# Expert ranking in one comparison and one product per 16 tiles, and four heads' scores in one group in the last attention steps

## The chip, the cores and the metric

The kernel runs on one core of a Trainium2 chip. The core has five engines that run their own instruction queues: PE (TensorE, matmuls; its weight loads are listed as PEld), DVE (VectorE), ACT (ScalarE), POOL (GpSimd) and SP (SyncE, which here only issues DMAs). The metric is the device time of one execution in microseconds. The kernel before took 4520.11 us as the median of three runs (4519.01 to 4522.6).

## The reference, cut to what matters

A macaron block over x of 4 x 2048 x 256, float32: a half feed-forward, an attention and another half feed-forward, each behind a layer norm and added to its input.

```python
x = x + 0.5 * _L0_ffn_ref(_layernorm(x), gate_w, w1, w2)
x = x + _L0_attn_ref(_layernorm(x), Wq, Wk, Wv, Wr, Wo)
x = x + 0.5 * _L0_ffn_ref(_layernorm(x), gate_w, w1, w2)
```

The feed-forward is a mixture of 8 experts of width 256. The router, for 8192 tokens:

```python
probs = softmax(xf @ gate_w.T)                  # [N, 8]
order = argsort(-probs); p_sorted = probs in that order
csum = cumsum(p_sorted); reached = csum >= 0.9, the last one always
k_idx = argmax(reached)                         # experts up to here are assigned
R = p_sorted - rank where assigned, else -1e9   # rank is 1 for the likeliest expert
keep = the 1024 tokens of largest R, per expert
scores_sel = probs where assigned and kept, else 0
```

The attention has 16 heads of 16 dimensions with causal masking; each head also has 4 "nodes" with softmax probabilities. They give rotary positions (running sums of the probabilities), and the score of two tokens has the logarithm of the product of their node probabilities added before the softmax.

## The kernel before, in words

Tokens are cut into 64 tiles of 128 rows. `experts` runs twice (before and after the attention), `attention` once; the three stages follow one another.

**The experts' first part** is a loop over groups of four tiles (line 303). `begin` loads 512 rows over SP's queue and takes their mean and variance on DVE (`bn_stats`, lines 185 and 186). `finish` normalises them (two of four tiles on ACT, line 206, and two on POOL, line 201), stores them by SP to the scratch tensor `normed`, transposes them on PE (line 215), copies the transposes out on ACT (line 219), multiplies them with the gate weights on PE (line 222) and copies the eight logits per token out (line 226). `spread` transposes these into `logits` (line 231), one group of tiles later.

After 16 tiles, `rank` works on 16 tiles at once: a softmax over 8 experts (maximum, difference, exponential on ACT, sum, reciprocal, product), and then, for each expert, which experts stand ahead of it. For that, each tile's 8 probabilities are written twice in a row: `twice` by POOL (lines 256 and 257), and `above` by DVE, with the second copy a hair larger (lines 258 and 259), so that ties fall as in the reference. Eight shifted windows of `above` are compared with the probabilities (line 263, DVE, eight instructions of 128 elements per partition for 16 tiles), and each result is multiplied by the shifted window of `twice` (line 266, POOL, eight instructions). `select` sums over the shifts (line 277: how many stand ahead; line 287: their summed probability), compares with the threshold and writes each token's key into `by_row` (line 293). It also cuts the probabilities into three bfloat16 parts on POOL (lines 280 to 285). `rank` is called in the loop at t = 16, 32 and 48 for 16 tiles each, at t = 60 for 12 tiles, and after the loop for the last 4 tiles; each `select` follows one round later. When all keys stand, PE transposes `by_row` (line 342) and a search of 14 rounds finds the key of rank 1024 per expert.

In this part the order of the instructions is not written out: a planner lists instructions engine by engine from their dependencies and its own estimates of cost; on the chip every queue is then worked off in that order. DVE, ACT and POOL thus stand still when the next instruction in their list waits.

**The attention** works in units of one sequence and four heads (16 units). A unit has four blocks of 512 queries, and a block has steps over tiles of 128 keys: `turns` lists them; the diagonal ones are the first (512 columns, masked), "two" (two pieces of 384 and 128 columns) and "one" (256 columns). A unit has 36 steps. `run` (line 1435) writes out the order by hand. In step n, for each of two pairs of heads, it issues

- `scores` of step n+1 for that pair (line 1077): two heads, each with a contraction of 32 rows of the array and a PSUM bank of its own, of the tag "sc", which has two buffers;
- `take`, the row maxima for later work, for the other pair (`maximum`, line 1144): two more heads in the other 32-row strips, with banks of the tag "mx", which has three buffers; DVE reads them;
- `weights`: the exponentials of the pair on ACT (`ex`), masked on POOL where the block is diagonal;
- `summed` (line 1103, into `acc`) and `summed_weights` (line 1120, into `den`) of step n, for half of the nodes and half of the columns, over all four heads;
- pieces of queued work (`normalise`, `project`, and the next unit's preparation), each of which takes one "mx" bank at a time.

`Metered` and `Clock` keep the planner's books for the queued work: an estimated time per engine, from which it decides which piece goes into which half step. `left` holds the maxima that are still to be taken; these run ahead of the scores, and `take` does nothing when its list is empty.

Of the kernel before, what the change touches and what calls it, by code (L numbers as in the profile page):

```python
# [14 lines left out]
ALU = mybir.AluOpType  # L15
# [4 lines left out]
P = 128  # L20
# [5 lines left out]
NX, FF = 8, 256  # L26
# [68 lines left out]
def macaron_kernel(  # L95
# [12 lines left out]
    nc = tc.nc  # L108
    N = x.shape[0]
    S = N // B  # L110
    NT = N // P
# [38 lines left out]
    def bcast(ap, shape):  # L150
        return ap.to_broadcast(shape)


    def experts(source, dst, base):

        GQ = min(4, ST)
        CH = 16
        V = 6
        full = [P, NT, NX]
        with tc.tile_pool(name="ffn", bufs=1) as pool, tc.tile_pool(  # L160
# [68 lines left out]
            def spread(t, turned):  # L229
                for i in range(4):  # L230
                    nc.tensor.transpose(
                        logits[:, t + i, :], turned[:, i * P : (i + 1) * P], ident[0:NX, 0:NX]
                    )

            def rank(c, m):

                some = [P, m, NX]
                pc = prob[:, c : c + m, :]
                one = pool.tile([P, CH], F32, name="one", tag="one", bufs=2)[:, 0:m]
                nc.vector.tensor_reduce(one, logits[:, c : c + m, :], AX.X, ALU.max)  # L240
                nc.vector.tensor_tensor(
                    pc, logits[:, c : c + m, :], bcast(one.unsqueeze(2), some), ALU.subtract
                )
                nc.scalar.activation(pc, pc, AF.Exp)
                nc.vector.tensor_reduce(one, pc, AX.X, ALU.add)
                nc.vector.reciprocal(one, one)
                nc.vector.tensor_tensor(pc, pc, bcast(one.unsqueeze(2), some), ALU.mult)

                ahead = pool.tile([P, CH, NX, NX], F32, name="ahead", tag="ahead", bufs=2)[:, 0:m]
                held = pool.tile([P, CH, NX, NX], F32, name="held", tag="held", bufs=1)[:, 0:m]
                twice = pool.tile([P, CH, 2 * NX], F32, name="twice", tag="twice", bufs=2)[:, 0:m]
                above = pool.tile([P, CH, 2 * NX], F32, name="above", tag="above", bufs=2)[:, 0:m]
                nc.gpsimd.tensor_copy(twice[:, :, 0:NX], pc)
                nc.gpsimd.tensor_copy(twice[:, :, NX:], pc)
                nc.vector.tensor_copy(above[:, :, 0:NX], pc)
                nc.vector.scalar_tensor_tensor(
                    above[:, :, NX:], pc, 1.5 * 2.0**-24, pc, ALU.mult, ALU.add  # L260
                )
                for d in range(NX):
                    nc.vector.tensor_tensor(
                        ahead[:, :, :, d], above[:, :, d : d + NX], pc, ALU.is_gt
                    )
                    nc.gpsimd.tensor_tensor(
                        held[:, :, :, d], ahead[:, :, :, d], twice[:, :, d : d + NX], ALU.mult
                    )
                return c, m, pc, ahead, held

            def select(c, m, pc, ahead, held):
# [24 lines left out]
                    sel.rearrange("p (r g) e -> p r g e", g=TPR), ALU.add,  # L296
                )


            ranks = {c + CH: (c, CH) for c in range(0, NT - CH, CH)}  # L300
            ranks[NT - 4] = NT - CH, CH - 4
            begun, flat, ranked = begin(0), None, None
            for t in range(0, NT, 4):
                now, begun = begun, begin(t + 4) if t + 4 < NT else None
# [4 lines left out]
                if ranked is not None:  # L309
                    select(*ranked)  # L310
                    ranked = None
                if t in ranks:
                    ranked = rank(*ranks[t])
            spread(*flat)
            select(*ranked)
            select(*rank(NT - 4, 4))

            def later(to, of):
                inst = nc.sync.dma_start(out=to, in_=of).ins
# [19 lines left out]
            ranked = pool.tile([P, W], F32, name="ranked")  # L339
# [283 lines left out]
    def attention():  # L623
# [43 lines left out]
        def bank(name, tag="mx"):  # L667
            if not gaps["steps"]:
                tag = turn_of.pop(0)
                turn_of.append(tag)  # L670
            return ps_rg.tile([P, 512], F32, name=name, tag=tag, bufs=BANKS[tag])
# [381 lines left out]
        def columns(at):  # L1053
            return 256 if at == "one" else 512
# [10 lines left out]
                return t[:, of[0] : of[0] + P].unsqueeze(1)  # L1065
            return t.rearrange("p (n w) -> p n w", w=P)[:, of[0] // P : of[1] // P + 1 : 3, :]

        def scores(u, ib, at, pair):

            q = u["qT"][ib]  # L1070
            out = [bank("sc", "sc") for _ in range(2)]
            for jt, off, n, to in pieces(ib, at):
                k = u["kT"][jt // 4]
                js = slice((jt % 4) * P, (jt % 4 + 1) * P)
                for j in range(2):
                    r = slice(32 * (2 * pair + j), 32 * (2 * pair + j) + 32)
                    nc.tensor.matmul(  # L1077
                        out[j][:, to : to + n], lhsT=k[r, js], rhs=q[r, off : off + n],
                        start=True, stop=True,
                    )  # L1080
            return out
# [182 lines left out]
        def maxima(ib):  # L1264
# [9 lines left out]
        left = {  # L1274
            pair: [(u, ib, at) for u in units for ib in range(NI) for at in maxima(ib)]
            for pair in range(2)
        }
# [6 lines left out]
        held = []  # L1284
# [129 lines left out]
        while units[0]["blocks"] < NI:  # L1414
# [6 lines left out]
            at = min(some, key=lambda at: max(known.get(id(behind[at]), (0, [0.0]))[1]))  # L1421
# [13 lines left out]
        def run():  # L1435
            for n, (u, ib, at) in enumerate(steps):
                if n == 0:
                    begin(span // 2 + 8)
                if ib == NI - 1 and at == turns[ib][0]:

                    begin(2 * n + span - 8)
                if n == 0:
                    for pair in range(2):
                        weights(scores(u, ib, at, pair), u, ib, at, pair)
                ex = dict(u["ex"])
                order(u, NI)
                while len(u["vn"]) <= max(jt for jt, _, _, _ in pieces(ib, at)) // 4:
                    advance(urgent, True)
                nxt = steps[n + 1] if n + 1 < len(steps) else None
                width = columns(nxt[2]) if nxt is not None else 512  # L1450
                if nxt is not None and nxt[2] == turns[nxt[1]][0]:
                    while nxt[0]["blocks"] <= nxt[1]:
                        onward(True)
                    ask(nxt[0], nxt[1])
                last = at == turns[ib][-1]
                for pair in range(2):
                    gaps["free"] = True
                    clock.now = max(clock.now, vec.end - LAG, act.end - LAG)
                    clock.now += 1.07 * width / 512
                    if nxt is not None:  # L1460
                        made = scores(*nxt, pair)
                    take(1 - pair, width)
                    if nxt is not None:
                        weights(made, *nxt, pair)
                    summed(u, ib, at, pair, ex)
                    if u is units[0] and ib > 0 and pair:

                        take(n % 2)
                    summed_weights(u, ib, at, ex, pair)
                    clock.now += 1.5 * columns(at) / 512  # L1470
                    if pair == 0:
                        if last:
                            while held:
                                advance(urgent, True)
                            got = [
                                pool.tile([P, 512], F32, name="oT", tag="oT", bufs=3)
                                for _ in range(3)
                            ]
                            act.copy(got[0], acc[0])
                        pass  # L1480
                    else:
                        if last:
                            act.copy(got[1], acc[1])
                            act.copy(got[2], den)
                            if u["g"] == 0:
                                outs[u["b"], ib] = pool.tile([P, 4, E], F32, name="o", tag="o", bufs=5)
                            held.append((id(u), ib))
                            urgent.append(normalise(u, ib, got))
                            if u["g"] == NG - 1:
                                urgent.append(project(u["b"], ib))  # L1490
                    if pair == 1 and ib == NI - 1:
                        after = units.index(u) + 1
                        if after < len(units):
                            order(units[after], sum(
                                turns[ib].index(at) >= max(
                                    m for m, o in enumerate(turns[ib])
                                    if any(jt // 4 == b for jt, _, _, _ in pieces(ib, o))
                                )
                                for b in range(NI)
                            ))  # L1500
                    if not advance(first):
                        advance(urgent)
                    pace(2 * n + pair)
            gaps["free"] = True
            while advance(urgent, True):
                pass

        with tc.manual_schedule():
            run()
# [45 lines left out]
```

## Time and profile before

| | |
|---|---|
| median of the runs | 4520.11 us (4519.01 to 4522.6) |
| the profiled execution's own time | 4516.34 us |
| its span, first to last instruction | 4514.5 us |
| mean granted TensorE clock | 0.94 |
| PE, DVE, ACT, POOL busy | 91%, 65%, 44%, 36% of the span |
| first experts' loop, first transpose to last logits | 11.3 to 87.4 us |
| attention's last steps without maxima | 4006.4 to 4101.8 us |
| second experts' loop, first transpose to last logits | 4131.4 to 4207.3 us |

A line of the timeline has the start in us, the time in us, the engine, the line of the kernel, the operation, what it writes and reads by the program's names, the shapes, how many instructions are merged, and in brackets the idle time of the engine just before and what ended it. A line of the stages has the stretch, its length, the busy time of PE, PEld, DVE, ACT and POOL with counts, the granted TensorE clock (1.00 is full), the busy share of the DMA engines and GB/s. An fp32 matmul shows as two instructions on PE.

### The profile page before, as it was taken

The page shows a single profiled execution, that of the slowest core. Times are in us where ns is not written, and L with a number is a line of the kernel's source. Part 1 is how long each engine was busy: PE and PEld are TensorE (multiplying, and loading weights), DVE is VectorE, ACT ScalarE, POOL GpSimd, SP SyncE. Part 2 cuts the span into 40 slices and gives each one's busy share as a digit, 9 for nine tenths or more (in the row PEclk, how much of TensorE's full clock was granted, in tenths as well). Part 3 has the DMA queues.
Part 4 walks back from the last instruction along what each step waited for, and adds up shares of the span by engine and source line. Part 5 has one row for each costly group of instructions (what it writes and reads, how often), then busy time and mean ns, then how long its engine had stood idle before and what let it go on. Part 6 is the DMA issues. An engine that isn't in the chain of part 4 may idle for free. (4 is left out here: it accounts for less than half of the span.)

```text
span 4514.5 us, 90151 instructions
## 1 busy us (share of the span) xinstructions
PE 4095.2 (91%) x36568; PEld 1834.3 (41%) x36568; DVE 2941.6 (65%) x7845; ACT 1969.1 (44%) x3821; POOL 1644.5 (36%) x2518
## 2 busy tenths in 40 slices
PE   6684698999999999999999999998999999997486
PEld 2453433434344444344444344443444444333254
DVE  6753575767676767676767676767576767533771
ACT  5333233435543545455434444454444444444432
POOL 4385323234233334241334242424242424112277
PEclk8696699999999999999999999999999999998688
DMA  7354000000100000001000000010000000004144
GB/s 246 81 84 85 1 1 1 1 1 2 39 15 15 29 1 2 1 2 38 15 29 15 1 2 1 2 38 15 29 15 1 2 1 2 1 29 140 70 75 76
DMA packets 108049, 136.30 MB, mean 30 GB/s; under 512 B 7792, under 2 KB 102256, under 8 KB 106480
## 3 DMA queue, kind: packets, MB, share of 16 engines
q1 hardware_dynamic: 81152, 95.84, 6.5%
q0 software_dynamic: 24576, 33.57, 4.5%
q8 instruction: 286, 4.69, 0.4%
q10 hardware_dynamic: 1904, 1.13, 0.1%
q14 instruction: 131, 1.07, 0.1%
HBM read 77.03 MB, written 61.87 MB: 31 GB/s over the span
## 5 line engine op out<-in xcount | busy, mean ns | idle before, releaser
L78 ACT ACTIVATE ex<-sc 128x512 f32<-128x512 f32 (+1 forms) x2304 | 1197.0, 572 | 1541.1 <-PE mx L1144 1326.8
L1144 PE MATMUL mx<-kT,qT 32*128 32x512 f32 (+3 forms) x5120 | 1349.8, 579 | 3.6 <-DVE top L78 3.1
L78 DVE TENSOR_REDUCE top<-mx 128x1 f32<-128x512 f32 x1536 | 1003.5, 684 | 468.2 <-PE mx L1144 462.4
L1077 PE MATMUL sc<-qT,kT 32*128 32x512 f32 (+3 forms) x5120 | 1288.0, 574 | 13.0 <-ACT ex L78 9.5
L1103 PE MATMUL acc<-ex,vn 128*32 128x512 f32 (+3 forms) x10240 | 1179.9, 541 | 0.8 <-POOL ex L78 0.8
L78 POOL TENSOR_SCALAR_AFFINE_SELECT ex<-ex 128x128 f32<-128x128 f32 (+1 forms) x768 | 255.6, 339 | 1275.5 <-ACT ex L78 1266.2
L78 DVE CUSTOM_DVE_ANT_0 mx<-mx,edge 128x128 f32<-128x128 f32 (+3 forms) x1024 | 498.7, 503 | 306.1 <-PE mx L1144 254.0
L1120 PE MATMUL den<-ex,share 128*4 128x256 f32 (+1 forms) x9216 | 672.2, 368 | 0.0
L1077 PEld LDWEIGHTS sc<-qT,kT 32*128 32x128 f32 x5120 | 424.1, 184 | 410.1 <-ACT ex L78 215.9
L1103 PEld LDWEIGHTS acc<-ex,vn 128*32 128x32 f32 x10240 | 215.8, 108 | 776.5 <-issue 711.8
L1144 PEld LDWEIGHTS mx<-kT,qT 32*128 32x128 f32 x5120 | 450.0, 186 | 73.7 <-DVE top L78 62.2
L1120 PEld LDWEIGHTS den<-ex,share 128*4 128x4 f32 x9216 | 244.7, 87 | 576.9 <-issue 548.9
L78 POOL TENSOR_TENSOR by_node<-by_node 128x512 f32<-128x512 f32 x64 | 86.3, 1348 | 521.7 <-DVE by_node L78 521.6
L78 POOL TENSOR_TENSOR vn<-v,share 128x1024 f32<-128x1024 f32 x64 | 124.5, 1950 | 238.0 <-PE acc L1103 236.5
L469 DVE TENSOR_SCALAR at<-row_b,low_t 128x128 bf16<-128x128 bf16 x992 | 174.2, 289 | 54.5 <-PE ps_l L470 42.2
L510 POOL DMA_INDIRECT xg<-normed,where x128 | 129.4, 1011 | 198.1 <-DVE sc L488 141.8
L558 PE MATMUL ps_o<-w,hT 128*128 128x256 f32 x512 | 147.3, 449 | 0.3 <-issue 0.2
L78 DVE DVE_READ_ACCUMULATOR2_ANT top<- 128x1 f32 x1024 | 144.4, 141 | 0.0
L78 DVE TENSOR_TENSOR by_node<-ps_o,tot 128x512 f32<-128x512 f32 x128 | 88.1, 690 | 71.8 <-PE ps_o L1186 59.4
L764 PEld LDWEIGHTS ps_a<-wa,xnT 128*128 128x128 f32 x1024 | 123.9, 197 | 26.4 <-ACT ex L78 13.5
L764 PE MATMUL ps_a<-wa,xnT 128*128 128x80 f32 x1024 | 133.4, 285 | 0.0
L78 POOL TENSOR_TENSOR prod<-turn,node 128x512 f32<-128x512 f32 x64 | 74.2, 1164 | 160.6 <-ACT turn L78 160.6
(230 smaller groups left out, 4841.6 us busy)
## 6 DMA issues: line engine op xcount, KB each, us to landing
xs<-x SPq DMA_DIRECT2D x32, 512.0 KB, 5.2
normed<-xn SPq DMA_DIRECT2D x32, 512.0 KB, 3.5
xs<-x SPq DMA_DIRECT2D x64, 256.0 KB, 2.7
w<-w SPq DMA_DIRECT2D x4, 2048.0 KB, 10.1
xs_o<-x SPq DMA_DIRECT2D x16, 512.0 KB, 3.9
x<-xs_o SPq DMA_DIRECT2D x16, 512.0 KB, 3.0
out<-xs_o SPq DMA_DIRECT2D x16, 512.0 KB, 4.1
xg<-normed,where POOLq DMA_INDIRECT x128
```

What stands on the lines that cost most here:

```text
L78: return getattr(self.engine, name)(*args, **kw)
L469: nc.vector.tensor_scalar(at[:, t, :], row_b, low_e, None, ALU.is_equal)
L510: inst = nc.gpsimd.indirect_dma_start(out=xg, out_offset=None, in_=normed, in_offset=bass.IndirectOffsetOnAxis(ap=lists[e][0][:, i : i + 1 ...
L558: nc.tensor.matmul(po[:, j, :], lhsT=hT[:, f, at : at + P], rhs=w2[:, f, e, :], start=f == 0, stop=f == 1,)
L764: nc.tensor.matmul(ps[:, j, :], lhsT=u["xnT"][:, c, (t + j) * P : (t + j + 1) * P], rhs=wa[:, c, u["g"], cols], start=c == 0, stop=c == 1,)
L1077: nc.tensor.matmul(out[j][:, to : to + n], lhsT=k[r, js], rhs=q[r, off : off + n], start=True, stop=True,)
L1103: nc.tensor.matmul(acc[half][32 * h : 32 * h + 32, off : off + n], lhsT=u["vn"][jt // 4][:, jt % 4, h, 32 * half : 32 * half + 32], rhs=ex ...
L1120: nc.tensor.matmul(den[32 * h : 32 * h + K, off + a - to : off + z - to], lhsT=u["share"][:, jt, h, :], rhs=ex[h][:, a:z], start=at == tur ...
L1144: nc.tensor.matmul(made[j][:, to : to + n], lhsT=q[r, i * P : (i + 1) * P], rhs=u["kT"][c][r, 0:n], start=True, stop=True,)
```

## The change

In `rank`, a helper `windows` describes all eight shifted windows of a doubled row by one access pattern: both of its inner dimensions have step 1, so that element (e, d) is element e + d of the row. One DVE instruction then compares all of them (1024 elements per partition for 16 tiles), and one DVE instruction makes all products with `twice`, which POOL did before. The last group of tiles is no longer ranked in 12 and 4: `rank` of tiles 48 to 63 runs once, after the loop.

In `attention`, `scores` takes one pair or both. In steps where no maxima are left to be taken, for either pair, `run` issues the scores of all four heads of the next step together, ahead of the first pair's `take`; the second pair's then lie in two "mx" banks, and in the second half step nothing is issued in their place. The exponentials stay where they were, and so do the books.

```diff
+            def windows(t):
+                return bass.AP(t.tensor, t.offset, [*t.ap[:2], [1, NX], [1, NX]])
...
-                for d in range(NX):
-                    nc.vector.tensor_tensor(
-                        ahead[:, :, :, d], above[:, :, d : d + NX], pc, ALU.is_gt
-                    )
-                    nc.gpsimd.tensor_tensor(
-                        held[:, :, :, d], ahead[:, :, :, d], twice[:, :, d : d + NX], ALU.mult
-                    )
+                nc.vector.tensor_tensor(
+                    ahead, windows(above), bcast(pc.unsqueeze(3), [P, m, NX, NX]), ALU.is_gt
+                )
+                nc.vector.tensor_tensor(held, ahead, windows(twice), ALU.mult)
...
             ranks = {c + CH: (c, CH) for c in range(0, NT - CH, CH)}
-            ranks[NT - 4] = NT - CH, CH - 4
...
             spread(*flat)
-            select(*ranked)
-            select(*rank(NT - 4, 4))
+            select(*rank(NT - CH, CH))
...
-        def scores(u, ib, at, pair):
+        def scores(u, ib, at, *pairs):
             q = u["qT"][ib]
-            out = [bank("sc", "sc") for _ in range(2)]
+            heads = [2 * pair + j for pair in pairs for j in range(2)]
+            out = [bank("sc", tag) for tag in ("sc", "mx")[: len(pairs)] for _ in range(2)]
             for jt, off, n, to in pieces(ib, at):
...
-                for j in range(2):
-                    r = slice(32 * (2 * pair + j), 32 * (2 * pair + j) + 32)
+                for j, h in enumerate(heads):
+                    r = slice(32 * h, 32 * h + 32)
...
+                four = nxt is not None and not any(left.values())
                 for pair in range(2):
...
-                    if nxt is not None:
+                    if four and pair == 0:
+                        made = scores(*nxt, 0, 1)
+                    elif four:
+                        made = made[2:]
+                    elif nxt is not None:
                         made = scores(*nxt, pair)
```

## The prediction

> **What bounds the kernel now.** I read the busy shares by slice first, then stages, then timelines of the two places that the change touches.
>
> ```profile
> PE   6684698999999999999999999998999999997486
> POOL 4385323234233334241334242424242424112277
> PEclk8696699999999999999999999999999999998688
> ```
>
> PE is full from slice 8 to 36, the attention; at both ends, the experts, it is not, and its clock falls there.
>
> ```profile
> 4006.00:4102.00 96.00, 95.80 (x800) 34.02 (x788) 6.45 (x13) 39.31 (x77) 7.07 (x18) 1.00 0.10 34
> ```
>
> In the attention's last 96 us PE is busy for 95.80, ACT for 39, DVE for 6: only PE time counts.
>
> ```profile
> 2001.61 0.70 PE L1077 MATMUL sc<-qT,kT 32*128 32x512 f32 x2
> 2001.63 0.70 PE L1144 MATMUL mx<-kT,qT 32*128 32x512 f32 x2
> 2002.15 0.59 PE L1077 MATMUL sc<-qT,kT 32*128 32x512 f32 x2
> 2002.16 0.59 PE L1144 MATMUL mx<-kT,qT 32*128 32x512 f32 x2
> 2002.68 1.07 PE L1103 MATMUL acc<-ex,vn 128*32 128x512 f32 x8
> ...
> 4081.40 1.13 PE L1077 MATMUL sc<-qT,kT 32*128 32x512 f32 x4
> 4082.46 1.06 PE L1103 MATMUL acc<-ex,vn 128*32 128x512 f32 x8
> 4083.34 0.61 PE L1120 MATMUL den<-ex,share 128*4 128x256 f32 x8
> 4083.89 1.13 PE L1077 MATMUL sc<-qT,kT 32*128 32x512 f32 x4
> ```
>
> From start to the next line's start, two heads of scores with two heads of maxima take 1.07 us (2001.61 to 2002.68), and two heads of scores alone 1.06 (4081.40 to 4082.46): alone, half of the array's strips idle.
>
> ```profile
> 54.21 3.06 DVE L263 TENSOR_TENSOR ahead<-above,prob 128x128 f32<-128x128 f32 x8
> 57.11 0.40 DVE L185 BATCH_NORM_STATS2 stats<-xs 128x6 f32<-128x256 f32 x1
> 57.43 1.20 DVE L277 TENSOR_REDUCE place<-ahead 128x128 f32<-128x1024 f32 x1
> 60.67 1.22 DVE L287 TENSOR_REDUCE sel<-held 128x128 f32<-128x1024 f32 x1 [2.05 <-POOL held L266]
> ...
> 63.45 1.97 PE L215 MATMUL ps_t<-cst,xn 128*128 128x128 f32 x8 [2.79 <-ACT xn L206]
> 66.10 3.58 PE L222 MATMUL ps_h<-xnT,wg 128*8 128x512 f32 x4 [0.15 <-ACT xnT L219]
> ...
> 86.82 0.59 PE L231 MATMUL logits<-cst,turned 8*128 8x8 f32 x4 [0.67 <-ACT turned L226]
> 100.05 1.12 PE L342 MATMUL ps_h<-cst,by_row 128*128 128x128 f32 x4 [12.63 <-DVE by_row L293]
> ```
>
> In the experts' loop DVE stands 2.05 us for POOL's products; the next rows' shift is queued behind, so ACT and POOL normalise late, PE idles 2.79 us, and then works at half clock. After the last logits PE waits 12.63 us for the rest of the ranking.
>
> **Part 1, ranking, per experts' stage (two alike).** Removed per 16 tiles: eight compares on DVE and eight products on POOL. Added: two DVE operations of 1024 elements, X us each. No row has X. Products of two float32 tensors of 512 elements in SBUF take 0.68 at least, compares of 128 take 0.20: 1.25 ns an element, so X = 1.32. The window pattern with a stretched operand has a relative in the lists' compare (line 444, two stretched inputs, bf16): 0.68 for 512, no penalty. But POOL works beside it: the same 512-element product reaches 1.57, 2.3 times, so X lies between 1.2 (the 1024-element sum, line 277) and 3.0. The eight compares together took 2.3 to 3.1 us against 1.6 for eight times the shortest, so they met POOL; with the products gone from POOL, less of that stays. I take 1.45.
>
> - Ranks at t = 16 and 32: first compare to the `held` sum takes 6.54 and 6.46 us now; after, 2X + 1.20 (`place` sum) + 0.40 (statistics between) = 4.5. Gain 2.0 each (2.5 with X = 1.2, a loss of 1.1 with 3.0). The new DVE product waits for POOL's second copy into `twice`, which ended at 54.44 while the compare would end at 55.7; if a 1.09 us pair of normalisations stands ahead of the copies, that is about 1 us late, and sums, statistics and the next shift are queued behind on DVE.
> - The clock: after the stalls (3.33 and 2.79 us) the granted clock was 0.57 from 42 to 50 us; eight transposes took 1.97 instead of 1.09 and four gate products 3.58 instead of 1.88, together 2.6 us. With the stall cut to about 1 us: a gap of 1.06 us (at 80.9) also came before gate products of 3.1 us at 0.50, so by this row nothing comes back; full return is 2.6. I take 1.3 for each of the two, keeping 0 and 2.6.
> - Rank at t = 48: its products stand in POOL's queue ahead of the last normalisation (81.33), for which PE idles 1.06 and then pays 1.2 for the clock. POOL without products: gain 1.06 + 0.6 = 1.7 (0 to 2.3).
> - End: the 12-tile rank, with all its DVE, ACT and POOL instructions, moves behind the last logits and merges with the 4-tile one. It issues no DMA and passes no load or store on SP; POOL's copies and splits (some 3 us) move with it, are read by the lists only later, and cost nothing. The path after the last logits: 2.1 to the compare (as 84.94 to 87.04), 2X = 2.9, two sums 2.4, small operations 1.5, hops 0.3: 9.2 against 12.6. Gain 3.4 (0.3 with X = 3.0, 3.9 with 1.2). Were Exp to need its table again (1.28 each), the gain shrinks by that.
>
> Sum 2 x 3.3 + 1.7 + 3.4 = 11.7. What is late next are row loads: from 15 to 30 us the DMA engines were full (share 0.98 to 1.05, 316 to 345 GB/s), and a load stands behind each store on SP's queue; DVE already waited 5.4 us for rows at 4145. I take 1.7 off: 10 per stage, 20 for both; bounds -2 and 16 per stage.
>
> On the clock, the Trainium skill's page TensorE: Matmul & The Clock Gate (Part 1: The HAM clock gate) says that the clock halves only after an idle window of about 3.4 us. By it, gaps of 1 us would leave the clock full and all 2.6 would return, an estimate of 2 x 1.3 x 2 = 5 us more over both stages; the row at 80.9 speaks the other way, so I stay between.
>
> **Part 2, four heads in one group.** The last maximum starts at 4004.5; 17 steps' scores follow without any: 15 of 512 columns ("two" among them), 2 of 256. Each now pays twice 1.06, or 0.63 twice; four heads take 1.07, or 0.64 (3950.55 to 3951.19). Gain 15 x 1.05 + 2 x 0.62 = 17.0. A full step shrinks from 4.97 to 1.07 + 2 x (0.88 + 0.55) = 3.93.
>
> The new wait: a group needs two "mx" banks besides two "sc"; with three buffers, one is still held by the last group until its third or fourth exponential. These end 1.16 + 4 x 0.5 = 3.2 us after the group's start, inside 3.93. Behind a waiting group on PE stand the sums of the first half, and ACT's copies of them at a block's end. It bites where ACT has more between: twice a projection's copy (0.58, waiting for PE) stands before the last two exponentials, about 0.3 each; at the last block's start four exponentials and three copies (3.8) meet a PE step of 2.6, about 0.4 worse than now. So 16; bounds 10 (0.4 lost in every step) and 17. The queued work keeps its half steps, for the books do not see the scores. Removed DVE or DMA work: none.
>
> **Sum.** 20 + 16 = 36 off the profiled execution's 4516.3 (span 4514.5): 4480. The median of the runs was 3.8 above it: 4484. Parts at their bounds give 4473 to 4496 where both work, taking the ranking as 20 give or take 9.
>
> **Rivals.**
> - R1: PSUM is emptied too slowly. If every full step waited for ACT as the last block's start does now (its two scores take 1.29 and 1.49 instead of 1.06: 0.66 in all), 17 becomes 17 - 15 x 0.66 = 7: 4493. For: three buffers for two tags' work. Against: ACT's 39 of 96 us, 49% of the 80 left. The Trainium skill's page TensorEngine Tiling (Array Packing), PSUM Bottleneck, warns of just this after fourfold tiling; the trace bears it out at the block's start only (ACT delays the scores there by 0.2 and 0.4 us).
> - R2: the loop is bound by its rows, or X nears 2.6, so ranking brings some 0 to 4: 4504. For: the full DMA slices. Against: over 11 to 88 us the DMA share is 0.60.
> - R3: the change does not do what it says: a remaining entry in the maxima's lists keeps the old path, and ranking gives nothing: 4520. Against: 4006 to 4102 us shows no maximum.
> - R4, slower: the overlapping windows cost DVE a restart every 8 elements. Without clock and with t = 48 unchanged at 1.7, a stage gains 2 x (4.9 - 2X) + 1.7 + 6.3 - 2X = 17.8 - 6X. With 16 from the attention, all is lost from X = 4.3 on; at 5.5, 128 restarts of 33 ns, the time is 4534. Nothing in the trace has such a cost; line 444 speaks against it.
>
> **How the numbers follow.** Forecast 0.75, R1 0.08, R2 0.09, R3 0.03, R4 0.05. The range 4472 to 4505 takes the forecast's spread, R1 and R2. A measurement tells 0.2% (9 us) from nothing, so faster 0.92 (forecast, R1, R2), same 0.03, slower 0.05. The likeliest case's own range is 4473 to 4496.
>
> **What would show it.** Per 16 tiles one compare and one product on DVE of 1.3 to 1.6 us and no idle time before the `held` sum; PE's gaps of 3 us in the loop near 1, clock above 0.57 after them; last logits to `by_row` 9 us. In the attention's end, score groups of eight instructions in 1.07 us, 17 times, and some 80 us from last maximum to last sums, not 97. Wrong it would be with X above 2.5, or with PE waiting for "ex" in each step.

## The result and the profile after

The changed kernel takes 4470.18 us (median, 4467.63 to 4474.51), the kernel before 4519.68 (4519.01 to 4522.6) beside it: a ratio of 0.9892, 95% interval 0.988 to 0.9903, 49.5 us less. The forecast was 36 less, and the time lies 2 us below the lower end of its range. The profiled executions took 4471.61 us (span 4469.9) and 4516.34 (span 4514.5): 44.7 less, and it is these 44.7 that the traces can divide.

| stretch, from milestones in the two traces (us) | before | after | difference |
|---|---|---|---|
| span's start to first transpose | 11.3 | 10.6 | -0.7 |
| first experts' loop, first transpose to last logits' end | 76.1 | 64.2 | -11.9 |
| last logits' end to `by_row` transposes | 12.6 | 8.8 | -3.9 |
| from there to the last maximum | 3904.4 | 3910.6 | +6.2 |
| last maximum to last sums (`acc`), start to start | 96.9 | 78.6 | -18.3 |
| from there to the second loop | 30.0 | 29.0 | -1.0 |
| second experts' loop | 75.9 | 65.8 | -10.1 |
| last logits' end to `by_row` transposes | 12.7 | 8.8 | -3.9 |
| from there to the end | 294.5 | 293.6 | -0.9 |

So both parts brought more than forecast (30 instead of 20, 18 instead of 16), and 6 us came back in between, which no step of the prediction had.

These are two executions. Five more traces below (the ranking alone, the two kernels with idle matmuls, the two with probes) have the changed kernel's instructions in the loops. Over the six, the first loop takes 64.2 to 66.1 us, 65.6 on average, and the second 63.9 to 66.9, 65.4 on average; with the old ranking, in two traces, they take 76.1 and 76.7, and 75.9 and 75.1. The changed kernel's own first loop is the shortest of the six. The wait ahead of the `by_row` transposes is 8.77 us in all of them.

The busy shares by slice of the changed kernel:

```profile
PE   6684698999999999999989999999899999997586
POOL 3485223334233334241333342413333424111277
PEclk8786699999999999999999999999999999998688
```

In slices of 112 us little is to be seen: POOL's first digit fell from 4 to 3 (its products there are gone) and its second rose from 3 to 4, the clock's first digit is 8 as before, and the middle is as full. The gain lies within slices. The timeline of the changed kernel at the rank of tiles 16 to 31 and at the end of the first loop:

```profile
48.07 0.34 POOL L260 COPY twice<-prob 128x128 f32<-128x128 f32 x1 [1.17 <-DVE prob L251]
48.59 1.23 DVE L267 TENSOR_TENSOR ahead<-above,prob 128x1024 f32<-128x1024 f32 x1
50.07 1.21 DVE L270 TENSOR_TENSOR held<-ahead,twice 128x1024 f32<-128x1024 f32 x1
50.56 1.88 PE L222 MATMUL ps_h<-xnT,wg 128*8 128x512 f32 x4 [1.89 <-ACT xnT L219]
51.19 1.21 DVE L279 TENSOR_REDUCE place<-ahead 128x128 f32<-128x1024 f32 x1
52.32 1.21 DVE L289 TENSOR_REDUCE sel<-held 128x128 f32<-128x1024 f32 x1
...
83.55 1.11 PE L341 MATMUL ps_h<-cst,by_row 128*128 128x128 f32 x4 [8.77 <-DVE by_row L295]
```

Compare and product are one instruction of 1.2 us each, the sum over `held` waits for nothing, the gate products take 1.88 us after a gap of 1.89 (before, 3.58 at 66.10), and PE waits 8.77 us at the end instead of 12.63. In the attention's end, by the view of stages and then by the timeline:

```profile
3996.00:4073.00 77.00, 77.00 (x792) 29.65 (x788) 6.11 (x13) 37.12 (x75) 7.03 (x18) 1.00 0.13 42
```

```profile
4053.24 1.14 PE L1077 MATMUL sc<-qT,kT 32*128 32x512 f32 x8
4054.31 1.07 PE L1103 MATMUL acc<-ex,vn 128*32 128x512 f32 x8
4055.20 0.61 PE L1120 MATMUL den<-ex,share 128*4 128x256 f32 x8
4055.63 1.04 PE L1103 MATMUL acc<-ex,vn 128*32 128x512 f32 x8
4056.49 0.61 PE L1120 MATMUL den<-ex,share 128*4 128x256 f32 x8
4057.03 1.14 PE L1077 MATMUL sc<-qT,kT 32*128 32x512 f32 x8
```

PE is busy for all of 77 us, ACT for 37. One step now takes 3.79 us (4053.24 to 4057.03): four heads' scores 1.07, sums 0.89 and 0.86, and the products with the shared weights (`den`) 0.43 where sums follow and 0.54 where scores follow.

### The profile page after: what moved, and what is told of

It reads as the page before. It is cut to its first block, busy times and chain, and to the rows that moved or that the text cites. A ratio compares the mean times of both kernels' runs of the same rounds, so it can differ in the third digit from the quotient of the medians.

```text
span 4469.9 us, 89976 instructions
## 1 busy us (share of the span) xinstructions
PE 4067.2 (91%) x36568; PEld 1827.8 (41%) x36568; DVE 2935.2 (66%) x7751; ACT 1968.8 (44%) x3819; POOL 1621.8 (36%) x2422
## 5 line engine op out<-in xcount | busy, mean ns | idle before, releaser
L1077 PE MATMUL sc<-qT,kT 32*128 32x512 f32 (+3 forms) x5120 | 1270.5, 575 | 13.0 <-ACT ex L78 9.5
```

The costliest lines, as they stand in the source:

```text
L1077: nc.tensor.matmul(out[j][:, to : to + n], lhsT=k[r, js], rhs=q[r, off : off + n], start=True, stop=True,)
```

## The experiments

Edits are against the changed kernel unless said. The runs were made on several chips, so each time stands to the kernel before on its own chip; that took 4514.7 to 4523.1 us.

### Each part alone

```diff
-                four = nxt is not None and not any(left.values())
+                four = False
```

> Only the ranking part is changed; the attention's last steps are issued pair by pair as before. Theory A (the parts add, and the miss lies in the experts' loops): the profiles place 16.5 us in the first experts' stage and 14.0 in the second, of which some 4 are lost again in the attention's opening, so 26 to 31 us off: 4489 to 4494. Rival B (the ranking gave the 20 that were forecast and the rest came from the attention): 4500.

In the other kernel the ranking is the old one (eight compares, eight POOL products, 12 and 4 tiles), and only the four-head scores remain.

> Only the attention's last steps are changed; the ranking is as before. Theory A: 18 us off, 16 forecast and 2 more because den is followed at once by the next acc: 4501 to 4502. Rival B: 25 to 30 us off, 4490 to 4495. In the profile a full step takes 3.79 us from score group to score group, not the 3.93 forecast.

The ranking alone: 4493.81 us, ratio 0.9942 (0.9928 to 0.9955), 24.2 less than the 4518.01 beside it. The scores alone: 4497.72 us, 0.9953 (0.994 to 0.9967), 20.3 less; from last maximum to last sums 78.6 us. The two add up to 44.5, so the parts do not help or hinder each other by more than the measurement sees. Both lie above their forecasts of 20 and 16, the scores by less than their interval. Without the new ranking the 6 us that came back are not lost: with the scores alone the last maximum starts at 4004.4, as before (4004.5).

### What of the ranking brings the gain

First the merging of the last group (ranked in 12 and 4 tiles again):

```diff
             ranks = {c + CH: (c, CH) for c in range(0, NT - CH, CH)}
+            ranks[NT - 4] = NT - CH, CH - 4
...
-            select(*rank(NT - CH, CH))
+            select(*ranked)
+            select(*rank(NT - 4, 4))
```

> As the changed kernel, but the last 16 tiles are still ranked as 12 and 4. Theory A (the end got shorter because DVE no longer waits for POOL; the merge is worth little, since the 12 tiles' rank of 7 us starts in DVE's idle time before the last logits): within 3 us of the changed kernel, 4468 to 4473, and PE's wait after the last logits is 8 to 9.5 us. Rival C (the merge itself gives the end's 3.9 us per stage): 4478, and the wait is about 12 us.

4472.74 us, ratio 0.9898 (0.9883 to 0.9914) where the changed kernel has 0.9892: the merging is worth nothing that can be measured, and the wait ahead of the `by_row` transposes is even shorter without it, 7.54 us instead of 8.77. With compares and products short, a rank of 12 tiles fits into the loop.

Then the one product back on POOL, as a single instruction:

```diff
-                nc.vector.tensor_tensor(held, ahead, windows(twice), ALU.mult)
+                nc.gpsimd.tensor_tensor(held, ahead, windows(twice), ALU.mult)
```

> As the changed kernel, but the one product of 1024 elements runs on POOL. A POOL product of 512 took 1.07, so 2.1 us here against 1.22 on DVE; the place sum (1.2) covers part. Theory A (DVE's wait for POOL is what counted): DVE waits about 1 us per rank, four ranks per stage, some 4 to 8 us back: 4474 to 4478. Rival D (what counted is that POOL's queue is free of products): about half of the ranking's gain is lost, 4483 or more.

4485.62 us, 0.9927 (0.9913 to 0.994): a third of the whole gain is gone, some 16 us. Its timeline:

```profile
35.36 2.29 POOL L270 TENSOR_TENSOR held<-ahead,twice 128x1024 f32<-128x1024 f32 x1
...
37.68 1.22 DVE L289 TENSOR_REDUCE sel<-held 128x128 f32<-128x1024 f32 x1 [2.27 <-POOL held L270]
...
40.47 0.70 PE L215 MATMUL ps_t<-cst,xn 128*128 128x128 f32 x4 [2.78 <-ACT xn L206]
42.77 3.35 PE L222 MATMUL ps_h<-xnT,wg 128*8 128x512 f32 x4 [0.67 <-ACT xnT L219]
```

This is the old stall in small: DVE waits 2.27 us for POOL, PE 2.78 for the rows behind it, and the gate products take 3.35 us. POOL's queue is longer here too, by the 2.29 us of the product, so this run does not tell DVE's wait from the queue.

The reverse: DVE has its own product, and POOL makes the eight old ones as well, into a tile that nobody reads. A float32 tile for all eight results does not fit (the pool then needs 207.7 KB per partition, and 204.1 are left), so the eight share a bfloat16 tile of 128 elements. At first that tile had the name of another one of the lists:

```diff
                 nc.vector.tensor_tensor(held, ahead, windows(twice), ALU.mult)
+                spare = pool.tile([P, CH, NX], BF16, name="spare", tag="spare", bufs=1)[:, 0:m]
+                for d in range(NX):
+                    nc.gpsimd.tensor_tensor(
+                        spare, ahead[:, :, :, d], twice[:, :, d : d + NX], ALU.mult
+                    )
```

> The changed kernel with the eight products of 128 elements kept on POOL as well, into a bf16 tile that nobody reads (it rounds what is thrown away): POOL has its old queue again, and DVE waits for none of it. Theory A (the gain came from DVE no longer waiting): at most the old 1.06 us gap at the last rows and a late normalisation return, 0 to 2 us per stage, 4470 to 4474. Theory B (the gain came in good part from a free POOL, which normalises half of the rows): the loop loses 3 us or more per stage, 4476 to 4486, with PE's gaps before the transposes ending on POOL's xn and gate products at 3.1 to 3.6 us.

4491.74 us, 0.9949 (0.9934 to 0.9964); but DVE waited 3.5 us per stage for POOL at the lists' own `spare`, ahead of the last rank's small operations, which hides the question; so next the tile has a name of its own, `unread`.

> As the run before with POOL's eight products kept, but their unread tile has a name of its own: the first had the name of a tile of the lists, so that DVE's first list operation waited 3.5 us per stage for POOL, ahead of the last ranking, and 4 us per stage of its 20 are of that. Theory B (POOL's queue of products stands ahead of its half of the normalisations, and freeing it is a good part of the gain): the end's wait is back at 8.8 us, the loop stays 5 to 8 us per stage longer than the changed kernel's, the time is 10 to 14 us above it: 4481 to 4485 where that has 4470. Theory A (only DVE's wait counts): the loop's loss goes with the name, 4470 to 4474.

4488.12 us, 0.9926 (0.9909 to 0.9943), some 16 us above the changed kernel: more than the 10 to 14 expected, by less than the interval, and far from theory A. DVE waits for nothing of POOL in the loop here, yet the loops take 70.9 and 71.0 us, 11 more together than the average of the six executions. The timeline at the first rank, and at the end of the loop:

```profile
36.85 4.93 POOL L273 TENSOR_TENSOR unread<-ahead,twice 128x128 bf16<-128x128 f32 x8
41.77 2.17 POOL L201 TENSOR_SCALAR xn<-xs,rstd,shift 128x256 f32<-128x256 f32 x4
42.38 1.54 PE L215 MATMUL ps_t<-cst,xn 128*128 128x128 f32 x6 [1.69 <-POOL xn L201]
44.59 3.58 PE L222 MATMUL ps_h<-xnT,wg 128*8 128x512 f32 x4 [0.68 <-ACT xnT L219]
...
89.32 4.17 POOL L273 TENSOR_TENSOR unread<-ahead,twice 128x128 bf16<-128x128 f32 x7
89.66 0.26 DVE L296 TENSOR_SCALAR place<-place 128x128 f32<-128x128 f32 x1
...
91.78 0.62 DVE L300 TENSOR_TENSOR by_row<-place,sel 128x128 f32<-128x128 f32 x1
92.46 1.12 PE L346 MATMUL ps_h<-cst,by_row 128*128 128x128 f32 x4 [10.05 <-DVE by_row L300]
```

POOL normalises two of four tiles, and its products stand ahead of that for 4.9 us; PE waits 1.69 us for POOL's `xn` and then needs 3.58 us for the gate products. DVE is slowed as well: beside the products some of its small operations take twice as long, and the end's wait is 10.05 us instead of 8.77. So with nobody waiting for them, the products keep some 16 of the 24 us that the ranking brings alone: freeing POOL was not the by-product that the prediction made of it. In the kernel before two things ended at the same place, DVE's wait for the products and POOL's queue of them. What the wait would cost without the queue no run shows.

Next, POOL's splits of the probabilities, which also stood in that queue, moved behind the last rank:

```diff
-                nc.gpsimd.tensor_scalar(rest, pc, 0.5, 0.0, ALU.mult, ALU.add)
-                for i in range(3):
...
             select(*rank(NT - CH, CH))
+            for c in range(0, NT, CH):
+                split(c, CH)
```

> The changed kernel with POOL's splits of the probabilities into three bf16 parts (six instructions, 4 to 5 us in each rank) taken out of the loop and issued behind the last ranking, 55 us before the lists first read them. Theory B (POOL's queue is on the loop's path): the normalisations that stand behind the splits come sooner, 1 to 3 us per stage, 4464 to 4468. Theory C (since the change ACT, with its two loads of function tables per rank, is what the loop waits for, POOL's splits lie beside it): within 1 us per stage, 4468 to 4472.

4470.6 us, 0.9892 (0.9876 to 0.9909): the changed kernel's own ratio, with loops of 65.5 and 65.8 us. The splits are off the path, as theory C has it; that ACT is what the loop waits for is not shown by this.

Last, what a microsecond of DVE costs in the loop:

```diff
+                for _ in range(3):
                     nc.vector.tensor_tensor(
                         ahead, windows(above), bcast(pc.unsqueeze(3), [P, m, NX, NX]), ALU.is_gt
                     )
```

> The changed kernel with its one compare issued three times: 2 x 1.22 us more of DVE in each rank, nothing else. Theory A (in the experts' loop DVE's queue is the bound at each rank, so each microsecond there ends on the path, and the clock stands behind it): the ranks at 16 and 32 and the one at the end lose 2.44 each, 7.3 per stage, and up to 2.6 per rank more where PE's gap falls to half clock: 15 to 25 us slower than the changed kernel, 4485 to 4495, the end's wait 11.2 instead of 8.77. Theory B (after the change the loop is bound by its rows, DVE has slack there): only the end pays, 2 x 2.44 = 5 us, about 4475, and the loop's 64 to 66 us do not move.

4495.73 us against 4523.12, ratio 0.9942 (0.9926 to 0.9959); the profiled span is 22 us above the changed kernel's: theory A. From its timeline:

```profile
48.01 3.34 PE L222 MATMUL ps_h<-xnT,wg 128*8 128x512 f32 x4 [1.92 <-ACT xnT L219]
...
71.93 3.33 PE L222 MATMUL ps_h<-xnT,wg 128*8 128x512 f32 x4 [1.89 <-ACT xnT L219]
...
94.75 1.12 PE L342 MATMUL ps_h<-cst,by_row 128*128 128x128 f32 x4 [11.48 <-DVE by_row L296]
```

The first `by_row` transposes come 11.2 us later than in the changed kernel, for 3 x 2.44 = 7.3 us of DVE on the path. From the first transpose on, and against the average of the six executions, it is 9.8 us: 1.3 us for each microsecond of DVE. The clock is in the excess, 1.46 us in each of the two slow gate products; five of the six executions have one such product in the first loop.

### What the loop waits for now

```diff
-                nc.scalar.activation(rstd, mv[:, :, 1], AF.Sqrt, bias=eps)
+                nc.scalar.activation(rstd, mv[:, :, 1], AF.Identity, bias=eps)
```

> The changed kernel with the experts' root of the variance taken as the variance itself (Identity in the place of Sqrt, so the rows are scaled by another number and the output is not the reference's): with it, Exp keeps its table and the five table loads of 1.28 us in each stage's loop are gone. Theory C (after the change ACT bounds the loop at each rank): PE's gap of 1.89 us ahead of the second rank's gate products falls below 1, the loop from the first transpose to the last logits gets 2 to 5 us shorter per stage, time 4460 to 4466. Rival (the rows bind it, as the prediction's discount of 1.7 us per stage has it): the loop stays at 64 to 66 us, and DVE waits for rows instead.

This kernel leaves out the square root. One run of 4472.08 us, where the changed kernel's ratio would give 4470.6. The second loop took 63.0 us (63.9 to 66.9 in the six executions), the first 68.5 (64.2 to 66.1), there with gate products of 3.37 and 3.45 us. Neither theory's numbers: without the table loads of 1.28 us PE's gap of 1.89 us is gone from both loops, as theory C said, but one loop is no more than 0.9 us below the shortest of the six, and the other lost more, in part to the clock. The rival's sign, longer waits for rows, did not show (5.1 us in the first loop, 5.5 in the changed kernel). What bounds the loop after the change stays open.

### The 6 us that came back

In the attention's opening, from the first transposes to the first scan of the running sums, the changed kernel needs 19.0 us and the kernel before 15.7. The timeline of before:

```profile
411.46 2.36 PE L764 MATMUL ps_a<-wa,xnT 128*128 128x80 f32 x20
413.65 1.99 PE L764 MATMUL ps_q<-wa,xnT 128*128 128x128 f32 x16
```

and of after, the same instructions:

```profile
395.87 4.39 PE L763 MATMUL ps_a<-wa,xnT 128*128 128x80 f32 x20
400.06 3.70 PE L763 MATMUL ps_q<-wa,xnT 128*128 128x128 f32 x16
```

That is 3.74 us, at a granted clock of 0.50 where before had 1.00. It is no fixed price of the faster ranking. Four traces have the same instructions up to the last maximum: the changed kernel's, that of the ranking alone, and the two with probes below. In them the opening took 19.0, 16.6, 19.5 and 15.6 us, with first query products of 3.70, 1.99, 3.70 and 1.99; and from the `by_row` transposes to the last maximum they took 6.2, 4.6, 2.0 and 3.0 us more than the kernel before. So what came back is 2 to 6 us, and differs from execution to execution. To see whether it is the clock and not the rows, matmuls that nobody reads were put into PE's wait ahead of the opening, first 52, then 29 of them:

```diff
         def turn_rows(xnT, t, xn):
+            if warm:
+                idle = ps_rg.tile([P, 512], F32, name="idle", tag="mx", bufs=BANKS["mx"])
+                for _ in range(warm.pop()):
+                    nc.tensor.matmul(
+                        idle, lhsT=ident, rhs=cst[:, 0:512], start=True, stop=True,
+                    )
```

> The changed kernel with 52 matmuls of 512 columns on constants, their product read by nobody, put on PE ahead of the attention's first transposes, into the 29 us in which PE waits there for rows. Theory (the ranking's 4 us that the attention's opening gives back are the clock: the 20 value products took 4.39 us instead of 2.36 and the 16 query products 3.70 instead of 1.99, at a granted clock of 0.50 instead of 1.00): the first eight transposes take about 1.1 us instead of 2.25, the value products 2.4, the query products 2.0, the opening's first scan starts near 402.5 instead of 407.1, and the whole is 3 to 5 us shorter, about 4466. Rival (the opening is bound by its rows and by ACT, and the slow products hide beside them): the scan stays at 406.5 to 407.5 and the time at 4470.

4482.34 us, 0.9908 (0.9892 to 0.9925). The 52 took 44.9 us and delayed the transposes by 17.5, yet the scan came only 10.0 late (417.1): at full clock, and with the rows long there, it took 11.6 us.

> As the run with 52 idle matmuls, but 29 of them: 52 took 44.9 us (two passes of 0.43 us each) and ended 17.5 us too late, so that run tells nothing of the rows. 29 fill about 26 us from 360.8 and end near 387, a microsecond ahead of the first transposes. Theory (the clock costs the opening its 4 us): transposes 1.1 us instead of 2.25, the 20 value products 2.2 to 2.4 instead of 4.39, the query products 2.0, first scan at 402 to 403.5, not 407.1; the whole 3 to 5 us shorter than the changed kernel, near 4466. Rival (rows and ACT bind the opening): scan at 406.5 to 407.5, time 4470.

4474.95 us, 0.9909 (0.9895 to 0.9922): no gain. The 29 ended at 385.6 and left PE idle for 4.59 us, so the first transposes ran at half clock after all (4 in 1.14 us). The last 16 value products then took 2.23 us (0.14 each, in the changed kernel 0.22), the query products 1.99, and the opening 16.3 us: 2.7 less than in the changed kernel, but no less than the 16.6 and 15.6 reached above without idle matmuls, so it is not shown to be their doing. All traces of the opening agree that the clock is the cause of most of it: with query products of 1.99 us it took at most 16.6 us, with 3.70 at least 19.0. Later the clock fell again (the second query products took 3.38 us), and the first maximum came at 482.5, the changed kernel's time, although this opening had begun 2.1 us later. So this push did not keep PE at full clock, and the gain is not to be had in this way. Of the changed kernel's 6 us, 0.7 were lost ahead of the opening and 1.8 behind the first maximum; these were not traced to a cause.

### The step of 3.79 us

Two kernels put a matmul of 2 columns ahead of the second half's sums in each four-head step, one in the scores' shape (32 rows), one in the sums' shape (128 rows, 32 columns of the array):

```diff
+                    if four and pair:
+                        probe = bank("probe")
+                        nc.tensor.matmul(
+                            probe[:, 0:2], lhsT=u["kT"][0][0:32, 0:P], rhs=u["qT"][ib][0:32, 0:2],
+                            start=True, stop=True,
+                        )
```

> The changed kernel, with one 2-column matmul of 32 rows (the scores' shape) ahead of the second half's sums in each of the 17 four-head steps, its product read by nobody. The question: in the tail the second product with shared weights takes 0.55 us when scores follow and 0.43 when sums follow, so the forecast step of 3.93 came out as 3.79. Theory (going between 32-row scores and 128-row sums costs PE about 0.12 us each time): the step grows by 0.2 us or more, the shared product ahead of the probe goes from 0.43 back to 0.55, last maximum to last sums 3 to 5 us longer than 78.8. Rival (0.12 is how the end of a group is counted, and no change of shape costs anything): the step grows by the probe's own 0.03 to 0.07 us, 0.5 to 1.2 in all, the same as with the probe in the sums' shape.

```diff
+                        nc.tensor.matmul(
+                            probe[0:32, 0:2], lhsT=u["vn"][0][:, 0, 0, 0:32], rhs=ex[0][:, 0:2],
+                            start=True, stop=True,
+                        )
```

> The control: a 2-column matmul in the shape of the sums (128 rows, 32 columns of the array) at the same place. Both theories: 0.03 to 0.07 us per step, 0.5 to 1.2 us in all; the shared product ahead of it stays at 0.43.

Last maximum to last sums: 78.6 us without, 80.9 with the sums' shape, 86.5 with the scores' shape. The step is 3.84 us with the former (4058.96 to 4062.80 in its timeline), 0.05 more; with the latter, in its timeline, from one group of scores to the next:

```profile
4061.85 1.14 PE L1077 MATMUL sc<-qT,kT 32*128 32x512 f32 x8
4062.92 1.06 PE L1103 MATMUL acc<-ex,vn 128*32 128x512 f32 x8
4063.80 0.61 PE L1120 MATMUL den<-ex,share 128*4 128x256 f32 x8
4064.34 0.38 PE L1473 MATMUL probe<-qT,kT 32*128 32x2 f32 x2
4064.65 1.07 PE L1103 MATMUL acc<-ex,vn 128*32 128x512 f32 x8
4065.53 0.61 PE L1120 MATMUL den<-ex,share 128*4 128x256 f32 x8
4066.08 1.14 PE L1077 MATMUL sc<-qT,kT 32*128 32x512 f32 x8
```

4.23 us, 0.44 more than 3.79: `den` ahead of the probe goes from 0.43 back to 0.54, and the probe itself takes 0.31 until the sums start. So a change of shape costs, there and back up to 0.4 us with so small a matmul between. Theory's direction, and more than its 3 to 5 us. The two probes differ in one thing more: the weights of the former are 32 columns wide and load in 0.11 us, those of the latter 128 columns and 0.18. How much of the 0.31 is that was not tested. The 0.54 of `den` does not hang on it: in the changed kernel the next group's weight loads start at 4055.41, while `den` still runs, where the shape stays, and where it changes only at 4057.03, with the group itself. The Trainium skill's page TensorEngine Tiling (Array Packing), Key Properties, says that a change of the tiling mode drains TensorE; the trace agrees with these starts, and has 0.54 us for `den` instead of 0.43.

## Why the prediction was off, point by point

- **What bounds the kernel:** right. The attention's end paid PE time and nothing else, and the loop's stall was DVE behind POOL, PE behind DVE, beside POOL's own queue.
- **X, the 1024-element operation:** taken at 1.45 us, measured at 1.22 and 1.22 (the compare 1.20 to 1.27, the product 1.20 to 1.42), at the lower bound. The overlapping windows cost nothing, so R4 fell, and with it the part of R2 that needed X of 2.6. The feared meeting with POOL went the other way: POOL waits, as told below.
- **The ranking, 10 us per stage forecast, 14.3 measured** (average of the six executions: 10.4 in the loop and 3.9 at its end). The step that failed most is "I take 1.7 off" for row loads: no such wait showed. In the first loop DVE waited for rows once for long, 5.5 us, as before (5.1), and not again after the ranks. The other terms that were off:
  - *Ranks at 16 and 32:* forecast 3.3 us each, 3.9 measured on average. On DVE, first compare to the `held` sum takes 3.84 and 3.73 us in the first loop instead of 6.54 and 6.46, so 2.7 each where 2.0 was forecast; X gives 0.46 of that. The clock's "1.3 for each", half of the full return, was about right on average: in the six executions 13 of the 24 gate products behind these ranks ran in 1.88 us, and 11 took 3.06 to 3.58. In the changed kernel's own first loop both were fast, and the ranks there gained 5.1 and 4.2; that was luck.
  - *Rank at 48:* forecast 1.7, measured 2.6 in the first loop.
  - *End:* forecast 9.2 us after the last logits, measured 8.77; gain 3.9 instead of 3.4, the difference being 2 x 0.23 of X. The reason was only half right: the old 12.6 came from the products, not from the split into 12 and 4, which could have stayed.
  - *POOL:* its freed queue was given value at the rank of 48 alone, while its products with nobody waiting cost 11 us in the two loops.
- **The attention's end:** forecast 16, measured 18.3, above its bound of 17. The step that failed is 3.93 us, which gave both shared-weight products the 0.55 they have in front of scores; in front of sums one takes 0.43. With 0.86 for the second sums, that is 0.14 us a step, in the 11 of 17 steps where the sums follow at once: 1.5. The rest is the 1.0 taken off for waits, of which only 0.1 showed: PE was busy for all of the 77 us, so R1 fell, and the one group that waited, at the last block's start, lost 0.75 where the two groups there had lost 0.66 before. The row that shows 0.43 was in the timeline of before:

```profile
4099.89 0.61 PE L1120 MATMUL den<-ex,share 128*4 128x256 f32 x8
4100.32 0.61 PE L1103 MATMUL acc<-ex,vn 128*32 128x256 f32 x8
```

- **R3:** the change did what it says; the timeline shows both forms.
- **What was not in the sum:** the 6 us given back from the first lists to the last maximum. In the two profiled executions the parts brought 12 us more than the sum had, 6 came back in between, and 2.6 more were gained around the loops (the table's small rows): 8.6 in all.
- **The median and the range:** the range had room for those 8.6, from 4484 down to 4472. What took the time out of it is the term "3.8 above": before, the median of the runs lay 3.8 us above the profiled execution, and the prediction carried that over; of the changed kernel it lies 1.4 below. That is the spread of the runs (4467.63 to 4474.51), and no property of either kernel. The narrower "4473 to 4496" does not follow from the parts either: with the ranking at its own bound of 16 per stage and the attention at 17 they reach 49 off, 4471, and the ranking's "20 give or take 9" has no working behind it.
- **The Trainium skill's page TensorE: Matmul & The Clock Gate** (Part 1: The HAM clock gate), whose rule would have added 5 us, was as far off as the row that I set against it: 13 of 24 is between the two. Gaps of 0.7 to 1.9 us came before products at full clock, as it says; gaps of the same 1.89 us also came before half clock, in the first loop in five of the six executions. The changed kernel has 1.88 us after such a gap (50.56, above); the kernel with 29 idle matmuls, the same program up to there, has, in its timeline:

```profile
51.33 3.39 PE L222 MATMUL ps_h<-xnT,wg 128*8 128x512 f32 x4 [1.89 <-ACT xnT L219]
```

The same section of the Trainium skill says that the window by which the clock is set runs freely and does not start anew with the kernel. That agrees with these pairs, the same instructions and the same gap at two clocks: the term is a chance between 0 and 1.5 us for such a gap, and no constant.

## What to carry to other kernels

When one engine waits for another that also has rows of its own to make, price both: the wait, and the queue that stands behind the work that is waited for. Take nothing off for a wait that no row shows. A term that hangs on TensorE's clock is to be kept as a chance per gap, with both ends in the range. One pair of traces is one draw of that chance: before a few microseconds are given a cause, compare several traces of the same instructions. When groups of different array shapes alternate, count the changes of shape too, for what follows an instruction is part of its price.

## What the runs showed of the hardware

- DVE's long operation holds POOL up, and POOL's products hold DVE's short ones up. Timeline of the changed kernel:

```profile
77.30 1.23 DVE L267 TENSOR_TENSOR ahead<-above,prob 128x1024 f32<-128x1024 f32 x1
77.40 1.28 POOL L282 TENSOR_SCALAR rest<-prob 128x128 f32<-128x128 f32 x1
78.63 1.23 DVE L270 TENSOR_TENSOR held<-ahead,twice 128x1024 f32<-128x1024 f32 x1
78.75 1.26 POOL L285 CAST part<-rest 128x128 bf16<-128x128 f32 x1
```

  POOL's two operations take 0.33 and 0.29 us at 32.23 and 32.62, where they meet none of DVE's long ones, and here as long as DVE's beside them; DVE's keep their 1.23. With POOL's eight products running (89.32 to 93.49 in the kernel with the unread products), DVE's last four small operations took 0.51 to 0.62 us each instead of 0.23 to 0.29, and the end's wait grew from 8.77 to 10.05. The Trainium skill's page SBUF — State Buffer (SBUF: two separate sides) describes a pair of ports that DVE, with two inputs in SBUF, and POOL hold in turn for a whole instruction; the trace agrees in both directions, for the compare and the product and for three of the four small operations, which have two inputs.
- PE at work without a pause doesn't bring the clock up within a fixed time. In the changed kernel's opening it was busy for 11.92 of the 12 us from 391.7 to 403.7, at 0.50 in all three windows of 4 us; in the kernel before the clock rose to 1.00 after some 4 us of the same work, and so it did with the probe in the sums' shape, whose instructions up to there are the changed kernel's. The Trainium skill's page TensorE: Matmul & The Clock Gate (Part 1: The HAM clock gate) gives about 3.4 us of sustained work for this; the 12 us here do not fit it.
